# A transformer layer on one core: the first group of tokens in a fixed order, its first block loaded in halves, the array warmed by matmuls

## The chip, the cores and the metric

The kernel runs on one core of one Trainium2 chip. The metric is the device time of one execution in microseconds (us); lower is better. The kernel before took 1701.09 us (median of three runs, 1698.03 to 1702.44).

## The reference

One layer with attention and a gated feed-forward part, each between two layer norms, on 2048 tokens of width 1024 in fp32:

```python
x = x + layernorm(attn(layernorm(x)))     # 4 * 256 -> q, k, v of width 256, one head, softmax, Wo
x = x + layernorm(ffn(layernorm(x)))      # silu(x Wg^T) * (x Wu^T), then Wd^T; hidden width 2752
```

## The kernel before, in words

Matmuls take fp32r operands. To keep fp32 accuracy every operand is split into a high part, which is a cast to fp32r, and a low part, the operand minus its high part; a product is then the sum of three matmuls (`mm3`) or, for v, of one 512-column and one 256-column matmul. `split` does the cast on ACT (L109) and the subtraction on DVE (L110).

The tokens are worked in four groups of 512 (`NG`), each of four blocks of 128 tokens (`TB`). For one block, `prep1` computes the row statistics (`norm_stats`: two `bn_stats` L116, `bn_aggr` L119, the addition of epsilon L120 on DVE, a power on POOL L121), normalises the block in place (L131 on DVE), transposes it by eight PE transposes (L139) into two PSUM banks, splits those into `xT`, and loads a block of the next group into the buffer that has come free. `v_block` forms v of a block from eight chunks of `wv` (L206 and L207), adds its bias (L210, L211 on DVE) and splits the result into `vt`. `qk` (L146 to L148) forms q or k of a whole group, 24 matmuls for each of four weight blocks.

Before the first product, `load_x` queues four blocks of x on SP, and `load_wv`, `load_wqk` queue weights on ACT, through two raw buffers (`wraw`) that both use in turn. At the very start 28 PE transposes of the identity (L216, `WARM`) keep the array busy.

A planner (the tile framework's scheduler with its own cost model) chooses the order of the instructions on each engine from the program, except where `tc.keep_in_program_order` fixes an instruction to its place. Before the change the first group is not fixed; the planner mixes its blocks with each other and with statistics of the second group. Engines execute their instructions in that order.

After the four groups come the scores of 128-query blocks (`scores`, a row maximum on DVE for each of four PSUM banks), the softmax (`softmax`: four exponentials on ACT from the four banks into `p_s`), transposes of `p_s` (`turn`), products with v (`attend`), the output projection, and then the feed-forward part, most of the time (L605). The weights `wo` are split into the buffer that held `wv`, once v is done. `scores(0)` and `softmax(0)` stand, in the program, just before the last group's four `v_block`s.

Of the kernel before, what the change touches and what calls it, by code (L numbers as in the profile page):

```python
# [10 lines left out]
AF = mybir.ActivationFunctionType  # L11
ALU = mybir.AluOpType
# [3 lines left out]
P = 128  # L16
T = 2048
C = 1024
D = 256
# [5 lines left out]
TB = G // P  # L25
# [3 lines left out]
EPS = 1e-5  # L29
# [5 lines left out]
def block_kernel(ctx, tc, x, wqk, wv, bqk, bv, wo, bo, wgu, wlast, wd, out):  # L35
# [12 lines left out]
    nc = tc.nc  # L48
# [4 lines left out]
    def tl(p, shape, dt, name):  # L53
        return p.tile(shape, dt, tag=name, name=name, bufs=1)
# [3 lines left out]
    ident = tl(cpool, [P, P], F32, "ident")  # L58
    make_identity(nc, ident)
    bqk_s = tl(cpool, [P, 4], F32, "bqk_s")  # L60
    bv_s = tl(cpool, [P, D], F32, "bv_s")
    bo_s = tl(cpool, [P, C], F32, "bo_s")

    mhalf = tl(cpool, [P, 16], F32, "mhalf")[:, 0:1]
    nc.vector.memset(mhalf, -0.5)

    ys = [tl(cpool, [P, 32], F32, f"ys{i}") for i in range(2 * TB)]
# [4 lines left out]
    def small_tile():  # L72
        small_n[0] += 1
        return small[small_n[0] % NSM]

    bank_pool = pool("banks", space=PSUM)
    bank = [tl(bank_pool, [P, 512], F32, f"bank{i}") for i in range(8)]
# [22 lines left out]
    qa = tl(rpool, [P, 2, 2, 512], F32R, "qa")  # L100
# [4 lines left out]
    def f32(ap):  # L105
        return ap.bitcast(F32)

    def split(hi, lo, src, lo_engine=None):
        nc.scalar.copy(hi, src)  # L109
        (lo_engine or nc.vector).tensor_tensor(lo, src, f32(hi), ALU.subtract)  # L110

    def norm_stats(halves, pin=None):

        s = small_tile()
        for i, h in enumerate(halves):
            b = nc.vector.bn_stats(s[:, 6 * i : 6 * i + 6], h)  # L116
            if pin:
                pin(b)
        nc.vector.bn_aggr(s[:, 12:14], s[:, 0:12])  # L119
        nc.vector.tensor_scalar(s[:, 14:15], s[:, 13:14], EPS, None, ALU.add)  # L120
        nc.gpsimd.tensor_tensor(s[:, 15:16], s[:, 14:15], mhalf, ALU.pow)  # L121
        return s[:, 12:13], s[:, 15:16], s

    def norm_rows(t, scalar):

        m, r, s = norm_stats([t[:, 0:512], t[:, 512:1024]])
        if scalar:
            nc.gpsimd.tensor_scalar(s[:, 16:17], m, r, -1.0, ALU.mult, ALU.mult)
            nc.scalar.activation(t, t, AF.Identity, bias=s[:, 16:17], scale=r)
        else:  # L130
            nc.vector.tensor_scalar(t, t, m, r, ALU.subtract, ALU.mult)  # L131

    def transpose_rows(t, dst, tb, banks):

        for hf in range(2):
            b = banks[hf]
            for j in range(4):
                cb = 4 * hf + j
                nc.tensor.transpose(b[:, j * P : (j + 1) * P], t[:, cb * P : (cb + 1) * P], ident)  # L139
            src = b.rearrange("p (j t) -> p j t", j=4)  # L140
            cols = slice(tb * P, (tb + 1) * P)
            split(dst[:, 4 * hf : 4 * hf + 4, 0, cols], dst[:, 4 * hf : 4 * hf + 4, 1, cols], src)
# [11 lines left out]
    vt = a1.rearrange("p a b c -> p (a b c)").rearrange("p (k h d) -> p k h d", h=2, d=D)  # L154
    xin, wraw, qst = f4[0:4], [f4[4], f2p[1]], f2[0:2]
    vst = [f2[4][:, 0:D], f2[4][:, D:]]
    wv_s = wvo.rearrange("p a b c -> p (a b c)").rearrange("p (k h d) -> p k h d", h=2, d=D)
    wqk_pool = pool("wqk", side="right")
    wqk_s = [tl(wqk_pool, [P, 8, 2, P], F32R, f"wqk{i}") for i in range(4)]
    x0_pool = pool("x0")  # L160
    xT = [tl(x0_pool, [P, 8, 2, G], F32R, "xT0"), a2]

    def load_x(t):
        nc.sync.dma_start(xin[t % TB], x[t * P : (t + 1) * P, :])

    raw_n = [0]
    WARM = 28

    def load_wqk(i):
        r = wraw[raw_n[0] % 2].rearrange("p (c f) -> p c f", f=P)  # L170
        raw_n[0] += 1
        nc.scalar.dma_start(r, wqk[i])
        split(wqk_s[i][:, :, 0, :], wqk_s[i][:, :, 1, :], r)

    def load_wv(i):
        r = wraw[raw_n[0] % 2].rearrange("p (c f) -> p c f", f=D)
        raw_n[0] += 1
        nc.scalar.dma_start(r, wv[:, 4 * i : 4 * i + 4, :])
        split(wv_s[:, 4 * i : 4 * i + 4, 0, :], wv_s[:, 4 * i : 4 * i + 4, 1, :], r)

    def prep1(t, banks):

        r = xin[t % TB]
        norm_rows(r, False)
        transpose_rows(r, xT[(t // TB) % 2], t % TB, banks)
        if t + TB < NT:
            load_x(t + TB)
# [11 lines left out]
            nc.scalar.activation(s, b, AF.Identity, bias=bqk_s[:, i : i + 1])  # L199
            nc.sync.dma_start(q_d[g][:, i - 2, :], s)  # L200

    def v_block(g, tb, b):
        xg = xT[g % 2]
        cols = slice(tb * P, (tb + 1) * P)
        for c in range(8):
            nc.tensor.matmul(b, xg[:, c, 0, cols], wv_s[:, c, :, :].rearrange("p a f -> p (a f)"), start=(c == 0), stop=False)  # L206
            nc.tensor.matmul(b[:, D:], xg[:, c, 1, cols], wv_s[:, c, 0, :], start=False, stop=(c == 7))  # L207
        k = g * TB + tb
        s = vst[tb % 2]
        nc.vector.tensor_tensor(s, b[:, :D], bv_s, ALU.add)  # L210
        nc.vector.tensor_tensor(s, b[:, D:], s, ALU.add)  # L211
        split(vt[:, k, 0, :], vt[:, k, 1, :], s)


    for _ in range(WARM):
        nc.tensor.transpose(bank[5][:, 0:P], ident, ident)  # L216

    load_x(0)
    load_wv(0)
    load_x(1)  # L220
    load_wv(1)
    load_x(2)
    load_x(3)
    nc.scalar.dma_start(bv_s, bv.partition_broadcast(P))
    nc.scalar.dma_start(bqk_s, bqk)
    for tb in range(TB):
        prep1(tb, (bank[2 * (tb % 2)], bank[2 * (tb % 2) + 1]))
        load_wqk(tb)
        v_block(0, tb, bank[6 + tb % 2])
    nc.scalar.dma_start(bo_s, bo.partition_broadcast(P))  # L230


    qraw = f4[4].rearrange("p (d q) -> p d q", d=2)
# [65 lines left out]
    def residual(t, a, xt):  # L299

        m, r, s = norm_stats([a[:, 0:512], a[:, 512:1024]], tc.keep_in_program_order if t >= EARLY else None)
        nc.gpsimd.tensor_scalar(s[:, 16:17], m, r, -1.0, ALU.mult, ALU.mult)
        nc.scalar.activation(a, a, AF.Identity, bias=s[:, 16:17], scale=r)
        (nc.gpsimd if t >= EARLY else nc.vector).tensor_tensor(xt, xt, a, ALU.add)
        nc.sync.dma_start(x1_d[t], xt)
        m, r, s = norm_stats([xt[:, 0:512], xt[:, 512:1024]])
        nc.gpsimd.tensor_scalar(s[:, 16:17], m, r, -1.0, ALU.mult, ALU.mult)
        nc.scalar.activation(a, xt, AF.Identity, bias=s[:, 16:17], scale=r)

    for g in range(NG):  # L310
# [24 lines left out]
    for tb in range(TB):  # L335
        v_block(NG - 1, tb, bank[6 + tb % 2])
# [43 lines left out]
    L, R = slice(0, 512), slice(512, 1024)  # L380
# [22 lines left out]
    pin = tc.keep_in_program_order  # L403
# [72 lines left out]
    class Slot:  # L476
        t = None
# [421 lines left out]
    for i in range(NT):  # L899
# [28 lines left out]
        cb = i - EARLY - 3  # L928
# [121 lines left out]
```

## Time and profile before

| | us |
|---|---|
| median of three runs | 1701.09 |
| the profiled execution, its own time | 1700.9 |
| its span in the profile | 1699.1 |
| PE busy | 1669.2 |
| DVE busy | 1100.3 |
| ACT busy | 694.8 |
| POOL busy | 91.3 |

The profile shows one execution. Start times are microseconds from the start of its span; about 1.8 us lie outside it. PE is the matmul engine and PEld its weight loads, DVE the vector engine, ACT the scalar engine, POOL and SP the other two; a trailing q is an engine's own instruction queue. A busy PE may still run at half its clock; the column PEclk tells the granted share.

### The profile page before, as it was taken

What the parts mean: (1) busy time and instruction counts of PE and PEld (TensorE: products, weight loads), DVE (VectorE), ACT (ScalarE), POOL (GpSimd) and SP (SyncE); (2) the same over time, 40 slices, a digit from 0 to 9 for tenths busy, and PEclk for the clock granted to TensorE, in tenths of its full rate; (3) what the DMA queues carried; (4) which work ended last, traced back from release to release, by engine and by line L of the source; (5) the groups of instructions that cost most, each with busy time, mean ns of one, the idle gap of its engine ahead of it and who ended that gap; (6) DMA issues with size and microseconds to landing.
All of it is one profiled execution on the core that took longest, in us unless ns stands there. A gap on an engine that the chain in (4) does not pass through costs nothing.

```text
span 1699.1 us, 21099 instructions
## 1 busy us (share of the span) xinstructions
PE 1669.2 (98%) x7764; PEld 1385.5 (82%) x7764; DVE 1100.3 (65%) x1682; ACT 694.8 (41%) x1039; POOL 91.3 (5%) x118
## 2 busy tenths in 40 slices
PE   8999999999899999999999999999999999999997
PEld 6888887888678888888888888788888888888886
DVE  8643667667787777776578457866555665455458
ACT  3222445544544444443365444433333333344343
POOL 1000000000011211110000000100000000000001
PEclk9999999999999999999999999999999999999999
DMA  6221123334676566665367666633332223566654
GB/s 214 81 81 38 38 75 121 101 118 169 218 243 209 200 215 212 217 220 183 122 204 252 215 191 198 210 106 113 130 111 100 93 94 124 209 221 192 195 189 158
DMA packets 131014, 271.00 MB, mean 159 GB/s; under 512 B 13280, under 2 KB 29792, under 8 KB 130912
## 3 DMA queue, kind: packets, MB, share of 16 engines
q1 hardware_dynamic: 128176, 262.72, 46.5%
q10 hardware_dynamic: 2736, 6.95, 1.2%
q8 instruction: 60, 0.98, 0.2%
q14 instruction: 42, 0.34, 0.1%
HBM read 185.73 MB, written 83.89 MB: 159 GB/s over the span
## 4 chain that ended last, share of the span: by engine, by line
PE 92%; DVE 4%; DMA 2%; ACT 1%; issue 1%; POOL 0%; SPq 0%; POOLq 0%; DVEq 0%; ACTq 0%
PE bank L605 69%; PE bank L146 4%; PE bank L147 4%; PE bank L148 4%; PE bank L276 3%; PE bank L277 2%; PE bank L206 2%; PE bank L268 1%; PE bank L207 1%; PE bank L347 1%; PE bank L139 1%; DVE a L110 1%; DVE small L116 0%; DMA f<-xT_d 0%; DVE wvo L110 0%
## 5 line engine op out<-in xcount | busy, mean ns | idle before, releaser
L605 PE MATMUL bank<-a 128*128 128x512 f32 x1164 | 274.2, 389 | 0.0
L605 PEld LDWEIGHTS bank<-a 128*128 128x128 f32 x1164 | 218.5, 188 | 45.3
L605 PE MATMUL bank<-xb,a 128*128 128x512 f32 x912 | 212.3, 389 | 0.1
L605 PEld LDWEIGHTS bank<-xb,a 128*128 128x128 f32 x912 | 171.1, 188 | 36.0 <-ACT xi L621 0.6
L618 DVE TENSOR_TENSOR xi<-bank,xi 128x512 f32<-128x512 f32 (+1 forms) x170 | 114.0, 682 | 115.0 <-PE bank L605 70.1
L110 DVE TENSOR_TENSOR a<-f2p,a 128x1024 fp32r<-128x1024 f32 (+2 forms) x133 | 134.6, 1012 | 58.0 <-ACT a L109 54.0
L109 ACT CAST a<-f2p 128x1024 fp32r<-128x1024 f32 (+2 forms) x133 | 117.5, 884 | 131.7 <-PE bank L605 107.2
L110 DVE TENSOR_TENSOR a<-f,a 128x1024 fp32r<-128x1024 f32 (+2 forms) x91 | 89.9, 988 | 106.5 <-ACT a L109 99.8
L605 PE MATMUL bank<-wvo 128*128 128x512 f32 x612 | 149.6, 389 | 0.0
L605 PE MATMUL bank<-kx,a 128*128 128x512 f32 x612 | 146.2, 389 | 0.0
L605 PE MATMUL bank<-a,a 128*128 128x512 f32 x588 | 140.2, 390 | 3.8 <-ACT xi L661 2.6
L605 PEld LDWEIGHTS bank<-kx,a 128*128 128x128 f32 x612 | 114.9, 188 | 23.8
L605 PEld LDWEIGHTS bank<-wvo 128*128 128x128 f32 x612 | 114.9, 188 | 23.9
L605 PEld LDWEIGHTS bank<-a,a 128*128 128x128 f32 x588 | 110.2, 188 | 27.5 <-ACT xi L661 3.0
L109 ACT CAST a<-f 128x1024 fp32r<-128x1024 f32 (+2 forms) x91 | 69.5, 764 | 141.6 <-PE bank L605 110.3
L605 PE MATMUL bank<-a,wvo 128*128 128x512 f32 x444 | 106.3, 389 | 0.0
L605 PE MATMUL bank<-kx,wvo 128*128 128x512 f32 x420 | 100.1, 389 | 0.0
L605 PEld LDWEIGHTS bank<-a,wvo 128*128 128x128 f32 x444 | 83.3, 188 | 17.3
L276 PE MATMUL bank<-a,a 128*128 128x512 f32 x256 | 94.6, 403 | 2.8 <-ACT f L349 2.0
L110 DVE TENSOR_TENSOR wvo<-f,wvo 128x1024 fp32r<-128x1024 f32 (+1 forms) x52 | 60.8, 1169 | 54.9 <-ACT wvo L109 53.8
L605 PEld LDWEIGHTS bank<-kx,wvo 128*128 128x128 f32 x420 | 78.8, 188 | 16.4
L618 DVE TENSOR_TENSOR xi<-xi,xi 128x512 f32<-128x512 f32 (+1 forms) x124 | 85.3, 688 | 5.6 <-ACT xi L621 1.5
(233 smaller groups left out, 2677.5 us busy)
## 6 DMA issues: line engine op xcount, KB each, us to landing
f2p<-wgu SPq DMA_DIRECT2D x41, 512.0 KB, 5.6
hd_S<-xi SPq DMA_DIRECT2D x80, 256.0 KB, 4.4
f<-x SPq DMA_DIRECT2D x30, 512.0 KB, 3.8
hd_A<-xi SPq DMA_DIRECT2D x60, 256.0 KB, 2.0
f<-wgu SPq DMA_DIRECT2D x22, 512.0 KB, 3.5
wr<-wgu SPq DMA_DIRECT2D x21, 512.0 KB, 5.9
f<-wd SPq DMA_DIRECT2D x20, 512.0 KB, 5.0
td_T<-f SPq DMA_DIRECT2D x40, 256.0 KB, 4.6
```

The costliest lines, as they stand in the source:

```text
L109: nc.scalar.copy(hi, src)
L110: (lo_engine or nc.vector).tensor_tensor(lo, src, f32(hi), ALU.subtract)
L139: nc.tensor.transpose(b[:, j * P : (j + 1) * P], t[:, cb * P : (cb + 1) * P], ident)
L146: nc.tensor.matmul(o, w[0], m[0], start=first, stop=False)
L147: nc.tensor.matmul(o, w[0], m[1], start=False, stop=False)
L148: nc.tensor.matmul(o, w[1], m[0], start=False, stop=last)
L206: nc.tensor.matmul(b, xg[:, c, 0, cols], wv_s[:, c, :, :].rearrange("p a f -> p (a f)"), start=(c == 0), stop=False)
L207: nc.tensor.matmul(b[:, D:], xg[:, c, 1, cols], wv_s[:, c, 0, :], start=False, stop=(c == 7))
L276: nc.tensor.matmul(b, p[:, k, 0, :], vt[:, k, :, :].rearrange("p h d -> p (h d)"), start=(k == 0), stop=False)
L277: nc.tensor.matmul(b[:, D:], p[:, k, 1, :], vt[:, k, 0, :], start=False, stop=(k == NKB - 1))
L605: one = nc.tensor.matmul(o, w[i], m[j], start=first and n == 0, stop=last and n == 2, skip_group_check=chained)
L618: nc.vector.tensor_tensor(o, a, b, op)
```

## The change

It touches the stretch before the second group, and with it the planner's order of what follows.

- The first block of x is loaded in two halves of 512 columns, one queued on SP and one on ACT. The two `wv` loads stay on ACT, behind that half. The bias loads `bv`, `bqk`, `bo` and the four `wqk` loads move from ACT's queue to SP's, where they stand among the loads of x.
- A copy of one column on ACT comes first, so that ACT's function table is loaded then. A second copy makes an fp32r copy of the identity, and 40 matmuls of 128 columns on it take the place of the 28 transposes.
- DVE, ACT and PE instructions of the first group, the POOL ones apart, are fixed in the order in which they are written. The first block is normalised in halves. Blocks 2 and 3 are normalised on ACT (`normed_scalar`) instead of DVE. The v products of a block are written as all 512-column matmuls and then all 256-column ones (block 0 in two runs of four chunks).
- `v_block` of the later groups keeps its form; `norm_rows` and `norm_stats` fix their DVE instructions where they are given `pin`, which `prep1` now does in every group. `norm_stats` now fixes its last two DVE instructions too, so the late `residual` calls, which passed `pin` before, have two more fixed ones.

```diff
     def prep1(t, banks):
         r = xin[t % TB]
-        norm_rows(r, False)
+        norm_rows(r, False, tc.keep_in_program_order)
...
-    WARM = 28
+    WARM = 40
...
     def load_wqk(i):
...
-        nc.scalar.dma_start(r, wqk[i])
-        split(wqk_s[i][:, :, 0, :], wqk_s[i][:, :, 1, :], r)
+        nc.sync.dma_start(r, wqk[i])
+        tc.keep_in_program_order(nc.scalar.copy(wqk_s[i][:, :, 0, :], r))
+        tc.keep_in_program_order(nc.vector.tensor_tensor(wqk_s[i][:, :, 1, :], r, f32(wqk_s[i][:, :, 0, :]), ALU.subtract))
...
+    def v_products(g, tb, b, c0, c1, run, pin=lambda i: i):
...
+        for h, c in [(h, c) for r in range(c0, c1, run) for h in range(2) for c in range(r, r + run)]:
+            if h == 0:
+                pin(nc.tensor.matmul(b, xg[:, c, 0, cols], wv_s[:, c, :, :].rearrange("p a f -> p (a f)"), start=(c == 0), stop=False))
+            else:
+                pin(nc.tensor.matmul(b[:, D:], xg[:, c, 1, cols], wv_s[:, c, 0, :], start=False, stop=(c == 7)))
...
-    for _ in range(WARM):
-        nc.tensor.transpose(bank[5][:, 0:P], ident, ident)
-    load_x(0)
-    load_wv(0)
-    load_x(1)
-    load_wv(1)
-    load_x(2)
-    load_x(3)
-    nc.scalar.dma_start(bv_s, bv.partition_broadcast(P))
-    nc.scalar.dma_start(bqk_s, bqk)
-    for tb in range(TB):
-        prep1(tb, (bank[2 * (tb % 2)], bank[2 * (tb % 2) + 1]))
-        load_wqk(tb)
-        v_block(0, tb, bank[6 + tb % 2])
-    nc.scalar.dma_start(bo_s, bo.partition_broadcast(P))
+    nc.sync.dma_start(xin[0][:, L], x[0:P, L])
+    nc.scalar.dma_start(xin[0][:, R], x[0:P, R])
+    load_x(1)
+    for i, r in enumerate(wraw):
+        nc.scalar.dma_start(r.rearrange("p (c f) -> p c f", f=D), wv[:, 4 * i : 4 * i + 4, :])
+    load_x(2)
+    load_x(3)
+    nc.sync.dma_start(bv_s, bv.partition_broadcast(P))
+    nc.sync.dma_start(bqk_s, bqk)
+    nc.scalar.copy(ys[0][:, 0:1], mhalf)
+    warm = qa[:, 0, 0, 0:P]
+    nc.scalar.copy(warm, ident)
+    for _ in range(WARM):
+        nc.tensor.matmul(bank[5][:, 0:P], warm, warm, start=True, stop=True)
...
+    def normed_scalar(tb, st):
+        m, r, q = st
+        nc.gpsimd.tensor_scalar(q[:, 16:17], m, r, -1.0, ALU.mult, ALU.mult)
+        pin(nc.scalar.activation(xin[tb], xin[tb], AF.Identity, bias=q[:, 16:17], scale=r))
...
+    st = stats(0)
+    normed(0, L, st)
+    normed(0, R, st)
+    turn_x(0)
+    split_wv(0)
+    turned(0, 0)
+    turned(0, 1)
+    v_products(0, 0, vb[0], 0, 4, 4, pin)
+    load_x(TB)
+    st = stats(1)
+    split_wv(1)
+    v_products(0, 0, vb[0], 4, 8, 4, pin)
+    normed(1, slice(0, C), st)
+    turn_x(1)
+    st = stats(2)
+    turned(1, 0)
+    turned(1, 1)
+    v_out(0, 0, vb[0], pin)
+    v_products(0, 1, vb[1], 0, 8, 8, pin)
+    load_x(TB + 1)
+    load_wqk(0)
+    normed_scalar(2, st)
+    turn_x(2)
+    st = stats(3)
+    turned(2, 0)
+    turned(2, 1)
+    v_out(0, 1, vb[1], pin)
+    v_products(0, 2, vb[0], 0, 8, 8, pin)
+    load_x(TB + 2)
+    load_wqk(1)
+    normed_scalar(3, st)
+    turn_x(3)
+    turned(3, 0)
+    turned(3, 1)
+    v_out(0, 2, vb[0], pin)
+    v_products(0, 3, vb[1], 0, 8, 8, pin)
+    load_x(TB + 3)
+    load_wqk(2)
+    v_out(0, 3, vb[1], pin)
+    load_wqk(3)
+    pin(nc.sync.dma_start(bo_s, bo.partition_broadcast(P)))
```

`turn_x` is the eight transposes of a block, `turned` the split of one of its two banks, `stats` is `norm_stats`, `normed` the DVE normalisation, `split_wv` the split of half of `wv`, and `v_out` the part of `v_block` behind its products; all are fixed in order by `pin`.

More of the change, by code (lines that the diff above doesn't have):

```diff
@@ L118, in norm_stats, with norm_rows @@
                 pin(b)
-        nc.vector.bn_aggr(s[:, 12:14], s[:, 0:12])
-        nc.vector.tensor_scalar(s[:, 14:15], s[:, 13:14], EPS, None, ALU.add)
+        b = nc.vector.bn_aggr(s[:, 12:14], s[:, 0:12])
+        if pin:
+            pin(b)
+        b = nc.vector.tensor_scalar(s[:, 14:15], s[:, 13:14], EPS, None, ALU.add)
+        if pin:
+            pin(b)
         nc.gpsimd.tensor_tensor(s[:, 15:16], s[:, 14:15], mhalf, ALU.pow)
         return s[:, 12:13], s[:, 15:16], s
-    def norm_rows(t, scalar):
-        m, r, s = norm_stats([t[:, 0:512], t[:, 512:1024]])
+    def norm_rows(t, scalar, pin=None):
+        m, r, s = norm_stats([t[:, 0:512], t[:, 512:1024]], pin)
         if scalar:
@@ L171, in load_wqk @@
         raw_n[0] += 1
-        nc.scalar.dma_start(r, wqk[i])
-        split(wqk_s[i][:, :, 0, :], wqk_s[i][:, :, 1, :], r)
[L175 to L179, printed above, removed]
+        nc.sync.dma_start(r, wqk[i])
+        tc.keep_in_program_order(nc.scalar.copy(wqk_s[i][:, :, 0, :], r))
+        tc.keep_in_program_order(nc.vector.tensor_tensor(wqk_s[i][:, :, 1, :], r, f32(wqk_s[i][:, :, 0, :]), ALU.subtract))
     def prep1(t, banks):
         r = xin[t % TB]
-        norm_rows(r, False)
+        norm_rows(r, False, tc.keep_in_program_order)
         transpose_rows(r, xT[(t // TB) % 2], t % TB, banks)
@@ L200, in qk @@
             nc.sync.dma_start(q_d[g][:, i - 2, :], s)
-    def v_block(g, tb, b):
+    def v_products(g, tb, b, c0, c1, run, pin=lambda i: i):
         xg = xT[g % 2]
         cols = slice(tb * P, (tb + 1) * P)
-        for c in range(8):
-            nc.tensor.matmul(b, xg[:, c, 0, cols], wv_s[:, c, :, :].rearrange("p a f -> p (a f)"), start=(c == 0), stop=False)
-            nc.tensor.matmul(b[:, D:], xg[:, c, 1, cols], wv_s[:, c, 0, :], start=False, stop=(c == 7))
+        for h, c in [(h, c) for r in range(c0, c1, run) for h in range(2) for c in range(r, r + run)]:
[3 more added lines that the diff above has]
+                pin(nc.tensor.matmul(b[:, D:], xg[:, c, 1, cols], wv_s[:, c, 0, :], start=False, stop=(c == 7)))
@@ L208, in v_block, with v_out @@
+    def v_out(g, tb, b, pin=lambda i: i):
         k = g * TB + tb
         s = vst[tb % 2]
-        nc.vector.tensor_tensor(s, b[:, :D], bv_s, ALU.add)
-        nc.vector.tensor_tensor(s, b[:, D:], s, ALU.add)
-        split(vt[:, k, 0, :], vt[:, k, 1, :], s)
-    for _ in range(WARM):
-        nc.tensor.transpose(bank[5][:, 0:P], ident, ident)
-    load_x(0)
-    load_wv(0)
+        pin(nc.vector.tensor_tensor(s, b[:, :D], bv_s, ALU.add))
+        pin(nc.vector.tensor_tensor(s, b[:, D:], s, ALU.add))
+        pin(nc.scalar.copy(vt[:, k, 0, :], s))
+        pin(nc.vector.tensor_tensor(vt[:, k, 1, :], s, f32(vt[:, k, 0, :]), ALU.subtract))
@@ L220, in block_kernel, with v_block @@
+    def v_block(g, tb, b):
+        v_products(g, tb, b, 0, 8, 1)
+        v_out(g, tb, b)
+    pin = tc.keep_in_program_order
+    L, R = slice(0, 512), slice(512, 1024)
+    nc.sync.dma_start(xin[0][:, L], x[0:P, L])
+    nc.scalar.dma_start(xin[0][:, R], x[0:P, R])
     load_x(1)
-    load_wv(1)
+    for i, r in enumerate(wraw):
+        nc.scalar.dma_start(r.rearrange("p (c f) -> p c f", f=D), wv[:, 4 * i : 4 * i + 4, :])
     load_x(2)
     load_x(3)
-    nc.scalar.dma_start(bv_s, bv.partition_broadcast(P))
@@ new lines, in hi, with lo, split_wv, turned @@
+    def hi(dst, src):
+        pin(nc.scalar.copy(dst, src))
+    def lo(dst, src, h):
+        pin(nc.vector.tensor_tensor(dst, src, f32(h), ALU.subtract))
+    def split_wv(i):
+        r = wraw[i].rearrange("p (c f) -> p c f", f=D)
+        w = wv_s[:, 4 * i : 4 * i + 4]
+        hi(w[:, :, 0, :], r)
+        lo(w[:, :, 1, :], r, w[:, :, 0, :])
+    def turned(tb, h):
+        b = bank[2 * (tb % 2) + h].rearrange("p (j t) -> p j t", j=4)
+        d = xT[0][:, 4 * h : 4 * h + 4, :, tb * P : (tb + 1) * P]
+        hi(d[:, :, 0, :], b)
+        lo(d[:, :, 1, :], b, d[:, :, 0, :])
@@ new lines, in turn_x, with stats, normed @@
+    def turn_x(tb):
+        for h in range(2):
+            for j in range(4):
+                cb = 4 * h + j
+                pin(nc.tensor.transpose(bank[2 * (tb % 2) + h][:, j * P : (j + 1) * P], xin[tb][:, cb * P : (cb + 1) * P], ident))
+    def stats(tb):
+        return norm_stats([xin[tb][:, L], xin[tb][:, R]], pin)
+    def normed(tb, h, st):
+        r = xin[tb][:, h]
+        pin(nc.vector.tensor_scalar(r, r, st[0], st[1], ALU.subtract, ALU.mult))
+    def normed_scalar(tb, st):
+        m, r, q = st
+        nc.gpsimd.tensor_scalar(q[:, 16:17], m, r, -1.0, ALU.mult, ALU.mult)
+        pin(nc.scalar.activation(xin[tb], xin[tb], AF.Identity, bias=q[:, 16:17], scale=r))
@@ new lines, in block_kernel @@
+    vb = bank[6:8]
+    st = stats(0)
[19 more added lines that the diff above has]
+    load_wqk(0)
```

## Prediction

> **What bounds the kernel now.** I read the page first: shares of busy time, then the slices.
>
> ```profile
> span 1699.1 us, 21099 instructions
> PE 1669.2 (98%) x7764; PEld 1385.5 (82%) x7764; DVE 1100.3 (65%) x1682; ACT 694.8 (41%) x1039; POOL 91.3 (5%) x118
> ...
> PE   8999999999899999999999999999999999999997
> ```
>
> PE is idle for only 1699.1 - 1669.2 = 29.9 us, so a change that leaves the matmuls alone moves time only through gaps of PE and its clock. Windows of 20 us place them: 6.4 us before 40 us, about 4 between 160 and 300, about 8.5 between 420 and 500, 1.3 near 1105, and the tail, 10.6. The first group is next, in windows of 5 us (columns: width, busy time and count of PE, PEld, DVE, ACT, POOL, then clock, DMA share, GB/s).
>
> ```profile
> 0.00:5.00 5.00, 3.64 (x17) 3.64 (x18) 0.06 (x1) 0.00 (x0) 0.70 (x6) 1.00 0.59 174
> 5.00:10.00 5.00, 2.96 (x19) 2.73 (x18) 3.15 (x6) 2.33 (x2) 0.55 (x1) 1.00 1.00 393
> 10.00:15.00 5.00, 3.75 (x13) 2.30 (x10) 5.00 (x9) 2.02 (x3) 0.00 (x0) 0.53 1.02 393
> 15.00:20.00 5.00, 4.03 (x19) 3.16 (x20) 5.00 (x14) 1.70 (x3) 1.97 (x3) 0.78 0.48 129
> 20.00:25.00 5.00, 4.87 (x33) 4.00 (x33) 5.00 (x10) 3.13 (x6) 1.64 (x2) 1.00 0.71 240
> 25.00:30.00 5.00, 4.33 (x28) 3.32 (x26) 5.00 (x11) 1.54 (x2) 0.00 (x0) 1.00 0.75 259
> 30.00:35.00 5.00, 5.00 (x24) 4.13 (x23) 4.59 (x9) 2.02 (x3) 0.00 (x0) 1.00 0.52 145
> ```
>
> DVE is full from 10 to 30 us and PE is full only from 30 on: DVE bounds the first group. The chain of waits says the same.
>
> ```profile
> 0.73 5.80 DMA f<-wv
> ...
> 6.92 1.28 ACT L109
> ...
> 8.21 1.05 ACT wvo L109
> ...
> 9.29 1.23 DVE wvo L110
> ...
> 25.62 0.60 DVE xT L110
> ...
> 26.26 0.39 PE bank L207
> ...
> 30.20 0.24 PE bank L147
> ```
>
> The wv load, the table load (6.92), the wv split, then DVE up to 26 us, then PE. The clock column (0.53, 0.78) shows the array at half speed from 10.3 to 17.1, which DVE hides.
>
> **What the Trainium skill says.** "TensorE: Matmul & The Clock Gate", Part 1, says that the array drops to half clock after an idle window of about 3.4 us and returns after a busy one. The trace agrees: half-microsecond windows put the drop at 10.3 and the return at 17.1, two such windows, although 28 transposes ran from 1.4 to 7.3. "ScalarE: Activation LUTs", What ACT_TABLE_LOAD costs, gives 1283 ns; here 1.28 us, and nothing of the drain that the page adds. "Trainium Kernel Development and Optimization", Key Constraints, says that SP's and ACT's transfers share the same 16 DMA engines; the trace has them at a share of 1.00 and 393 GB/s, so two queues alone add no bandwidth.
>
> **The change, part by part.** I walk the first group in its new fixed order with durations of before: statistics 1.28 + 0.20 + 0.15 and 0.55 on POOL; DVE normalisation 0.81, ACT's (L303) 1.24; casts 1.05 (1024 columns), 0.59 (512, PSUM), 0.41 (256); subtractions 1.22, 0.69, 0.42; v's two additions 0.41 + 0.40; PE 0.23 per 512 columns, 0.87 for eight transposes, and about 0.2 until the last result. Neighbours on DVE and ACT overlap by 0.1; a semaphore costs 0.05.
>
> Loads. The DMA engines had moved 0.52 MB by 3.9 us and 1.57 MB by 6.95, and a landing is seen about 0.45 later. With x's halves first on both queues, block 0 lands at about 4.4 (was 6.1), the first wv half, now behind it and level with block 1, at 7.4 (was 6.5). The table load, moved ahead of the data, takes 1.28 off the wv cast: 7.4 instead of 8.2. Warming: after three DMA issues on ACT (to 2.1), the table load and two short copies, the fp32r copy is ready at about 3.9; 40 matmuls at a cold 0.107 (the 768 cold columns at 12.7 took 0.64) end by 8.2.
>
> Block 0 is normalised at 6.8 to 7.5, transposed from 8.2; the first v half waits for wv's subtraction until 9.8. DVE then runs without a gap: two subtractions, statistics, second wv subtraction to 13.65. The second v half starts at 13.75, block 1's transposes at 15.1, its v ends at 19.4. For blocks 2 and 3 a loop forms: transposes, cast, two subtractions, v's additions on DVE, then on ACT, in order, the v cast, the wqk cast (1.05) and the normalisation (1.24) before the next transposes. The waiting normalisation holds PE; POOL's two added products end at 17.3 and 23.9, before ACT is free for it. The loop gives transposes at 21.0 and 27.1, 6.1 apart, and block 3's v products at 28.5.
>
> Before, at 30.20, all but block 3's v and 94 of 96 q/k products was done, with eight transposes of group 2 (0.87) and two q/k matmuls (0.46) beyond; the equal state is at 28.87. The start gains 0.4. If block 0 lands only at 6.0, the walk gives 29.1, a loss of 0.2; a wv half at 6.5 gives 28.0, a gain of 0.9.
>
> Clock. Between the two v halves PE now idles from 11.4 to 13.7. I charge 1.0, between 0 and 4: a half-clock window of 3.4 us costs up to 1.7 where PE bounds, and two can fall in this stretch. The 28 transposes removed and the 40 matmuls hide under the loads.
>
> SP's queue: wqk loads wait there for raw buffers, group 2's x loads behind them. wqk 0 to 3 issue at 9.8, 13.7, 21.1 and 27.2 and are needed at 18.7, 24.9, 30.8 and 35.3; x of block 4 is needed only at 39. Both are costed at nothing, hidden by that slack; without it, 4 to 5 us of landing would show. The later bo load serves the attention projection, first used at 196 us: nothing.
>
> Later groups. Group 2's statistics now follow on DVE at 39; PE wants that block at 46. In the built order of group 3, its last block's normalisation stands behind a v addition, two residuals and a POOL power; my walk has it 0.7 late, its cast 0.4 more: 1.0 lost, from 0 to 2.
>
> **Start of attention.** Here the planner's new order matters most. Before, the first softmax ran under v products:
>
> ```profile
> 157.12 0.39 PE L148 MATMUL bank<-kx,qa 128*128 128x512 f32 x1
> ...
> 158.66 0.69 ACT L259 ACTIVATE p_s<-bank,ys 128x512 f32<-128x512 f32 x1 [5.13 <-DVE ys L257]
> ...
> 162.99 0.60 PE L268 MATMUL bank<-ident,p_s 128*128 128x128 f32 x4
> ```
>
> In the changed program the last scores stand behind all q/k products, with nine v matmuls left as cover:
>
> ```
> PE:  scores(0,3) x5; v block 15 x9; turn(0,0)
> DVE: max of bank3; wo half 0 low; v 15 add; wo half 1 low; softmax scale
> ACT: q casts; wo half 0/1 high; exp(0,0)
> ```
>
> With 0 at the first of the five scores, they end at 1.15 and v at 2.65. ACT's second wo cast needs v's sixth chunk, 2.2, and ends at 3.3; DVE, after the v addition at 3.7, subtracts until 4.85, scales until 5.05; the exponential takes 0.69, so the transposes start near 5.85. PE waits 3.1 us. Before, PE lost 0.9 around 178 here; I let that go: net 2.2, from 0 to 3.5. The rest of attention keeps a steady order with 4.8 us of PE work over each softmax; nothing, give or take 2.
>
> Sum against the profiled execution: -0.4 + 1.0 + 1.0 + 2.2 = +3.8, so 1700.9 + 3.8 = **1704.7 us**. The profiled time stands 0.2 below the median. The start lies within about 5.1 us, 0.3%, which is what a measurement of this kernel can tell from no change.
>
> **Rivals.** *No change that can be told* (0.47): the sum above, with own range 1699 to 1706.
>
> *Slower* (0.38): the array falls to half clock in the first group. The page's 10.3 to 17.1 speaks for it: 40% busy in the window before was too little. The new order leaves 11.4 to 13.7 empty and pauses of 1.6 and 1.8 us before blocks 2 and 3. Against it, 40 matmuls leave it warm at 8.2. A cold window on the transposes of block 1 costs 2.1 through the loop, one at 28 us costs 1.7: 3.8 in place of 1.0 gives 1700.9 + 6.6 = 1707.5. It decides from 2.3 us of clock loss on.
>
> *Faster* (0.15): the planner's new order removes gaps of attention, 0.9 near 178 and 3.1 between 200 and 300, and one of the 1.6 waits between 420 and 500, adds none, the array stays warm and wv lands at 6.5: 1700.9 - 0.9 - 4.0 - 1.6 = 1694.4. The cover that I miss at attention's start speaks against it.
>
> *Not what it says*: the halves may not land earlier; the wv split bounds then as now, so that costs the 0.6 between 28.5 and 29.1, within the first case.
>
> **How the numbers follow.** Faster by over 0.3%: 0.15; within: 0.47; slower: 0.38. The range reaches from the faster case's near edge, 1696.5, to the slower case with attention's upper bound, 1707.5 + 1.3 and 1 of other gaps: 1710.
>
> **What would show it.** In the profile after: PE full from 28 to 29; the wv cast at 7.4 with no table load ahead; the transposes of blocks 2 and 3 released by ACT, 6 us apart; PE waiting about 3 us for p_s near 160; the clock column near 14. Wrong if PE is full by 25 us, if no wait of over 1 us stands ahead of the first p_s transposes, or if the gaps between 420 and 500 change by over 3 us.

## The result, and the profile after

Over six executions each, the changed kernel took 1707.61 us (median; 1705.73 to 1709.31) and the kernel before 1699.20: a ratio of 1.0043 with a 95% interval of 1.003 to 1.0056, so 0.43% slower. (The ratios in this document are the recorded estimates over the single executions; dividing these two medians would give 1.0049.) The profiled execution after took 1707.8 by its own time, 6.9 more than the profiled one before, where the prediction's sum was +3.8.

The page after, its lines on the span, on busy time and PE's slices:

```profile
span 1705.7 us, 21134 instructions
PE 1676.1 (98%) x7776; PEld 1393.2 (82%) x7776; DVE 1099.5 (64%) x1681; ACT 698.7 (41%) x1043; POOL 90.1 (5%) x120
...
PE   8999999999999999999999999999999999999997
```

PE's idle time is 1705.7 - 1676.1 = 29.6 us, against 29.9 before. By the page nothing was gained or lost in waiting: PE is busy 6.9 us longer, although the layer's own matmuls are the same. The extra busy time is in the 40 warm matmuls, which last longer than the 28 transposes did, and in matmuls at half clock. This is the first thing to see: a busy share cannot tell work from filler.

The first group after, in windows of 5 us (columns as in the prediction):

```profile
0.00:5.00 5.00, 1.13 (x5) 1.13 (x6) 0.79 (x3) 1.67 (x3) 0.70 (x6) 1.00 0.63 213
5.00:10.00 5.00, 5.00 (x25) 5.00 (x25) 2.06 (x6) 1.05 (x1) 0.55 (x1) 1.00 0.95 340
10.00:15.00 5.00, 5.00 (x23) 4.68 (x23) 1.77 (x2) 1.15 (x3) 0.00 (x0) 1.00 0.59 208
15.00:20.00 5.00, 2.90 (x12) 2.27 (x11) 4.43 (x8) 0.97 (x2) 1.48 (x1) 0.90 0.42 120
20.00:25.00 5.00, 5.00 (x24) 4.30 (x24) 3.47 (x8) 1.30 (x3) 0.82 (x2) 0.76 0.48 161
25.00:30.00 5.00, 3.12 (x19) 2.43 (x18) 4.09 (x8) 3.45 (x5) 0.70 (x2) 0.92 0.39 127
30.00:35.00 5.00, 4.48 (x22) 3.55 (x20) 2.72 (x6) 3.12 (x5) 0.12 (x1) 0.74 0.45 132
```

DVE, which was full from 10 to 30 us before, is nowhere full. PE is full from 5 to 15, and DVE is busy for only 2.06 and 1.77 of 5 us there. PE is full for good only from 35, where it was 30 before. The timeline of PE says what it does (start, length, line, tiles, shape, count; in brackets the idle time ahead and what ended it):

```profile
3.87 8.80 PE L240 MATMUL bank<-qa 128*128 128x128 f32 x40 [3.87 <-ACT qa L238]
12.47 1.93 PE L265 MATMUL bank<-ident,f 128*128 128x128 f32 x8
14.22 1.80 PE L207 MATMUL bank<-wvo,xT 128*128 128x512 f32 x4
...
18.58 1.75 PE L207 MATMUL bank<-wvo,xT 128*128 128x512 f32 x4 [2.10 <-DVE wvo L246]
...
20.98 1.73 PE L265 MATMUL bank<-ident,f 128*128 128x128 f32 x8
...
27.43 1.10 PE L265 MATMUL bank<-ident,f 128*128 128x128 f32 x8 [1.65 <-ACT f L277]
28.77 3.42 PE L207 MATMUL bank<-wvo,xT 128*128 128x512 f32 x8 [0.24 <-ACT xT L243]
...
33.68 1.09 PE L265 MATMUL bank<-ident,f 128*128 128x128 f32 x8 [0.30 <-ACT f L277]
35.02 1.20 PE L207 MATMUL bank<-wvo,xT 128*128 128x512 f32 x4 [0.24 <-ACT xT L243]
```

DVE's timeline has the normalisation of block 0:

```profile
6.66 1.00 DVE L272 TENSOR_SCALAR f<-f,small 128x512 f32<-128x512 f32 x2 [0.67 <-POOL small L125]
```

The 40 matmuls take 8.80, 0.22 each. Block 0 was normalised by 7.66, so its transposes (L265) are 4.8 late, and no bracket tells so, since PE was not idle: work in front of other work on the same engine is a wait that no list of waits contains. When they do start they run at half speed, 1.93 for eight, where a full clock gives about 1.0. The chain of waits puts the matmuls on the path, and shows further on what stands between the blocks:

```profile
3.87 8.80 PE bank L240 x40
12.67 1.74 PE bank L265 x8
...
25.19 1.05 ACT wqk L177
26.27 1.22 DVE wqk L178
27.49 1.21 DVE small L116 x2
...
31.45 1.04 ACT wqk L177
32.49 1.15 ACT f L277
...
33.68 0.67 PE bank L265 x4
```

Block 3's v products start at 35.02. The equal state of the kernel before was at 28.87, so the start costs 6.15. At the start of attention, just before 180 us, the list of PE's waits (waited for, us in total, times, longest) has:

```profile
PE bank L358 <- ACT p_s L349: 2.8, 1, 2.8
```

### The profile page after: what moved, and what is told of

The parts are those of the page before. It is cut to its first block, busy times and chain, and to the rows that moved or that the text cites. A ratio compares the mean times of both kernels' runs of the same rounds, so it can differ in the third digit from the quotient of the medians.

```text
span 1705.7 us, 21134 instructions
## 1 busy us (share of the span) xinstructions
PE 1676.1 (98%) x7776; PEld 1393.2 (82%) x7776; DVE 1099.5 (64%) x1681; ACT 698.7 (41%) x1043; POOL 90.1 (5%) x120
## 4 chain that ended last, share of the span: by engine, by line
PE 90%; DVE 4%; DMA 2%; ACT 2%; issue 1%; ACTq 0%; POOL 0%; DVEq 0%; SPq 0%; POOLq 0%
PE bank L695 67%; PE bank L150 4%; PE bank L152 4%; PE bank L151 4%; PE bank L366 3%; PE bank L367 2%; PE bank L358 1%; PE bank L207 1%; PE bank L437 1%; PE bank L209 1%; DVE a L110 1%; PE bank L143 1%; PE bank L240 1%; DMA f<-xT_d 0%; DVE wvo L110 0%
## 5 line engine op out<-in xcount | busy, mean ns | idle before, releaser
L110 DVE TENSOR_TENSOR a<-f2p,a 128x1024 fp32r<-128x1024 f32 (+2 forms) x133 | 134.5, 1012 | 58.9 <-ACT a L109 55.1
L110 DVE TENSOR_TENSOR a<-f,a 128x1024 fp32r<-128x1024 f32 (+1 forms) x75 | 83.2, 1109 | 105.6 <-ACT a L109 99.0
L109 ACT CAST a<-f 128x1024 fp32r<-128x1024 f32 (+1 forms) x75 | 63.0, 840 | 110.7 <-PE bank L695 110.3
L110 DVE TENSOR_TENSOR wvo<-f,wvo 128x1024 fp32r<-128x1024 f32 (+1 forms) x51 | 59.5, 1167 | 53.8 <-ACT wvo L109 53.1
```

## The experiments

The theory after the result: the warm matmuls hold PE past the moment at which it has real work, and the loss at attention's start is a second cost that stands by itself. The rivals: the loop through ACT would hold the start whatever the warming, or the warming was needed and the slow array is the cost. A time below is a median, a ratio is against the kernel before, timed on the same chip. Some differences between two runs are of medians from different chips; the kernel before took 1698.96 to 1699.58 on these, so a few tenths in them mean nothing. "Cover" is work that an engine can do in a stretch in which it would otherwise wait.

**Run 1: fewer warm matmuls.**

```diff
-    WARM = 40
+    WARM = 18
```

> 18 warm matmuls instead of 40; every other instruction of every engine stands where it stood in the changed kernel. Theory A (the warm matmuls hold PE past the moment at which block 0 is normalised): at 0.22 each they end near 7.9 instead of 12.7, block 0 is transposed at about 8.0 (12.47 with 40), block 3's v products start some 3 to 5 us earlier than 35.0 (30 to 32), and the time falls by 3 to 5 us below the changed kernel. Rival B (the loop through ACT, in which the normalisation of blocks 2 and 3 stands behind a v cast and a wqk cast, sets the start): the first transposes move, but block 3's v stays within 1 us of 35.0 and the time within 1 us. Rival C (the 40 matmuls are what keeps the clock up later): the clock column shows more half-speed windows before 35 us and the time rises by 1.7 for each.

Measured: 1702.36 us, ratio 1.0016 (1.001 to 1.0023), 5.3 below the changed kernel. PE's timeline:

```profile
3.88 4.11 PE L240 MATMUL bank<-qa 128*128 128x128 f32 x18 [3.88 <-ACT qa L238]
7.78 1.93 PE L265 MATMUL bank<-ident,f 128*128 128x128 f32 x8
...
24.42 1.09 PE L265 MATMUL bank<-ident,f 128*128 128x128 f32 x8 [1.64 <-ACT f L277]
...
30.69 1.09 PE L265 MATMUL bank<-ident,f 128*128 128x128 f32 x8 [1.87 <-ACT f L277]
32.02 1.19 PE L207 MATMUL bank<-wvo,xT 128*128 128x512 f32 x4 [0.24 <-ACT xT L243]
```

Block 0 is transposed 4.7 earlier and block 3's v starts 3.0 earlier, with the same order of instructions on every engine but for one product of the scores near 187 us. Theory A holds, with both numbers at the edge of what was expected; rival C falls, since the time went down. The loop (rival B) is not all of it, but 32.02 is still 3.15 behind the kernel before, so it can be the rest.

Only 3.0 of the 5.3 is seen at the start. Set side by side, the two profiles keep this distance to about 445 us; it is 3.9 at 470, 4.1 at 1080 and 5.9 at 1112, behind a wait of 1.2 that the changed kernel has and this run lacks. Run 2 has such a wait (1.0). Why the later gaps differ isn't shown.

**Run 2: none at all** (`WARM = 0`).

> No warm matmul at all; the order of the rest is the changed kernel's but for a handful of places. Theory A: block 0 is transposed at about 7.8, the array is at half clock there exactly as with 40 (0.215 a transpose), block 3's v starts within 1 us of the kernel with 18, and the time within 1.5 us of it: the warm matmuls buy nothing. Rival C (they do warm the array, late): the first release of the clock comes 3 us or more later than with 18, and the time is 1.7 to 3.4 us above it.

Measured: 1703.10 us, ratio 1.0024 (1.0016 to 1.0032). Block 0 is transposed at 7.39, again in 1.97, and block 3's v starts at 32.00. The matmuls on the identity bought nothing that these intervals can tell (theory A; rival C wanted at least 1.7 more than run 1).

**Runs 3 and 4: cover for the first softmax.** The v products of the last group held behind the four scores on PE, with 40 and with 18 warm matmuls:

```diff
     for tb in range(TB):
-        v_block(NG - 1, tb, bank[6 + tb % 2])
+        v_products(NG - 1, tb, bank[6 + tb % 2], 0, 8, 1, pin)
+        v_out(NG - 1, tb, bank[6 + tb % 2])
```

> The v products of the last group are held on PE behind all four scores of the first turn, as they stood in the kernel before; the warm matmuls stay at 40. Theory: the 2.8 us for which PE waits for the first p_s goes (under 0.3), and with it the half-clock window after it (0.91 between 170 and 190 us), so the time falls by 2.8 to 4.5 us below the changed kernel, while the start stays as it was (block 3's v at 35.0). Rival: the wait only moves to the next turn, or to the v copies of the last group that attention needs, and the time falls by less than 1 us.

> 18 warm matmuls and the held v products together. If the start and the start of attention are two independent costs, the gains of the two single edits add: 6 to 9 us below the changed kernel, that is 1699 to 1702 us, level with the kernel before. If attention absorbs either (as it gave back about 4 us of what was lost ahead of it in the changed kernel), the sum falls short by 2 us or more.

Measured: 1713.34 us, ratio 1.0073 (1.0061 to 1.0085), and 1707.84, 1.0044 (1.0032 to 1.0056). Both lose 5.5 to 5.7 against their partner without the cover. The wait for p_s did go, but in the list of PE's waits of the first of them, between 100 and 180 us, stand:

```profile
PE bank L150 <- DVE a L110: 2.6, 1, 2.6
PE bank L143 <- DVE f L135: 1.8, 2, 1.5
```

As I read these waits, the v products had covered the casts before the first scores, and moved behind them they left that place open. Besides, PE's idle time between 180 and 300 us, 0.3 in the changed kernel, is 3.8. The theory of a cost that can be bought off alone fell.

**Run 5: the normalisation first.** With 18 warm matmuls. `v_out` is cut into its additions on DVE (`v_adds`) and the copy and subtraction (`v_keep`), so that ACT's normalisation can stand ahead of the copy and of the wqk cast:

```diff
     turn_x(1)
-    st = stats(2)
+    st2, st3 = stats(2), stats(3)
     turned(1, 0)
     turned(1, 1)
-    v_out(0, 0, vb[0], pin)
+    normed_scalar(2, st2)
+    v_adds(0, 0, vb[0], pin)
     v_products(0, 1, vb[1], 0, 8, 8, pin)
     load_x(TB + 1)
-    load_wqk(0)
-    normed_scalar(2, st)
     turn_x(2)
-    st = stats(3)
     turned(2, 0)
     turned(2, 1)
-    v_out(0, 1, vb[1], pin)
+    normed_scalar(3, st3)
+    v_adds(0, 1, vb[1], pin)
+    v_keep(0, 0, pin)
+    load_wqk(0)
...
```

> 18 warm matmuls, and in the fixed order ACT's normalisation of blocks 2 and 3 stands directly behind the xT casts of the block before it, ahead of v's copy and the wqk cast; statistics of block 3 follow those of block 2. Theory A (with the warming out of the way it is this loop that sets the start): from the durations of the kernel with 18, transposes of block 2 at 22.4 (24.4 there), of block 3 at 26.4 (30.7), block 3's v products at 27.6 (32.0), which is 1.3 before the equal state of the kernel before; the time falls by 3 to 5 us below the kernel with 18, to 1697 to 1699.5. Rival B (the slow array sets the start, not the order): block 3's v moves by less than 2 us. Rival C (PE is earlier at block 3 but then waits for wqk casts that now stand later): idle of PE between 28 and 40 rises by what the start gains.

Measured: 1698.41 us, ratio 0.9998 (0.9989 to 1.0006), 4.0 below run 1. Its PE timeline:

```profile
22.00 1.04 PE L272 MATMUL bank<-ident,f 128*128 128x128 f32 x8
...
26.19 1.03 PE L272 MATMUL bank<-ident,f 128*128 128x128 f32 x8
27.46 1.20 PE L207 MATMUL bank<-wvo,xT 128*128 128x512 f32 x4 [0.24 <-ACT xT L250]
```

No bracket stands before the transposes any more: PE no longer waits for ACT. 22.00, 26.19 and 27.46 against the expected 22.4, 26.4 and 27.6. Rival C falls too: PE's idle time between 28 and 40 us, 2.1 in run 1, is nothing here. The order on ACT was the second cost of the start, hidden behind the first. This run, which has fewer warm matmuls and the new order on ACT, is back at the time of the kernel before.

**Run 6: the early table load alone, in the kernel before.**

```diff
+    nc.scalar.copy(ys[0][:, 0:1], mhalf)
     for _ in range(WARM):
```

> The kernel before, with one more ACT copy ahead of the first loads' use, so that the table is loaded at once; no other instruction moves on any engine. If the table load (1.28 at 6.92 in the chain of waits) is worth what the chain shows, the wv cast goes to 6.9, DVE's row of work starts 1.28 earlier and the time falls by about 1.3. My theory: nothing (within 0.3 in the profile's start, the wv subtraction still at 9.3), because DVE's normalisation of block 0, which stands ahead of that subtraction and ends at 9.31, is as late as the cast is.

Measured: 1698.61 us, ratio 1.0 (0.9991 to 1.001). Its wv cast stands at 7.21, 1.0 earlier, and DVE's timeline is:

```profile
8.84 0.81 DVE L131 TENSOR_SCALAR f<-f,small 128x1024 f32<-128x1024 f32 x1 [0.67 <-POOL small L121]
9.56 1.22 DVE L110 TENSOR_TENSOR wvo<-f,wvo 128x1024 fp32r<-128x1024 f32 x1
```

The subtraction (L110) starts the moment DVE is through with the normalisation, and not earlier than before (9.29), although its cast had been done for 1.3 us. (Block 0's statistics started 0.34 later in this execution, 6.45 against 6.11, which is why it is even a little later.) The chain of waits shows one path; a second one, here DVE's statistics and normalisation, was exactly as late.

**Run 7: the old warming in the changed kernel.** 28 transposes of the identity instead of the 40 matmuls.

```diff
-    WARM = 40
+    WARM = 28
...
-        nc.tensor.matmul(bank[5][:, 0:P], warm, warm, start=True, stop=True)
+        nc.tensor.transpose(bank[5][:, 0:P], ident, ident)
```

> The changed kernel, warmed by the 28 transposes of the identity that the kernel before used instead of 40 matmuls; the planner orders later groups somewhat differently, so the start is what is read. Theory A (the transposes release the clock and, needing no copy, start at 1.4 and end by 7.4): block 0's eight transposes start at 7.7 and take 1.0, not 1.93; block 1's start near 16.8 (17.8 with 18 matmuls) and take 0.9 to 1.0, block 3's v products start at 30 to 30.5, 1.5 to 2 earlier than with 18 matmuls. Rival B (PE's idle stretches between 9 and 15 make it slow again whatever came first): block 1's transposes take 1.7 to 1.9 and block 3's v starts within 0.7 of 32.0.

Measured: 1705.34 us, ratio 1.0038 (1.0024 to 1.0053). Its PE timeline:

```profile
1.35 5.33 PE L240 MATMUL bank<-ident 128*128 128x128 f32 x28 [1.35 <-POOL ident masks.py:199]
7.10 1.11 PE L265 MATMUL bank<-ident,f 128*128 128x128 f32 x8 [0.41 <-DVE f L272]
...
15.97 1.91 PE L265 MATMUL bank<-ident,f 128*128 128x128 f32 x8
...
28.86 1.39 PE L265 MATMUL bank<-ident,f 128*128 128x128 f32 x8 [1.87 <-ACT f L277]
30.19 2.07 PE L207 MATMUL bank<-wvo,xT 128*128 128x512 f32 x4
```

Both theories were half right: the transposes release the clock (block 0's take 1.11), PE then idles for 2.3 us twice and block 1's are slow again (1.91). Block 3's v starts at 30.19, 1.8 ahead of run 1, but its products run at half speed, so that the q/k product that follows at 34.90 there follows at 34.34 here: 0.6 is left. The time is nevertheless 3.0 above run 1. The largest difference between the two profiles is in attention, which the planner put in another order. Three windows of 120 us tell it, the changed kernel, the kernel before, and this run:

```profile
180.00:300.00 120.00, 119.74 (x659) 101.47 (x658) 78.99 (x168) 61.46 (x129) 8.99 (x22) 0.99 0.23 77
```

```profile
180.00:300.00 120.00, 116.94 (x645) 98.11 (x645) 80.54 (x167) 59.47 (x123) 9.80 (x24) 1.00 0.25 80
```

```profile
180.00:300.00 120.00, 117.07 (x641) 98.54 (x641) 79.19 (x164) 57.67 (x119) 8.67 (x21) 1.00 0.23 72
```

PE's idle time there is 0.3, 3.1 and 2.9 us. Runs 1, 2 and 5, in which the planner's order stays close to the changed kernel's, have 0.3 at most; this run has the wait of 2.8 for p_s as well as the gaps. So the order of attention that came with the change saves 2.8, and it isn't the price of the wait ahead of it.

**Runs 8 and 12: what the warm matmuls do to the clock.** In the changed kernel, 20 of 512 columns (run 8, four copies of the identity side by side), and 40 of 256 (run 12, two copies). The edit of run 12:

```diff
-    nc.scalar.copy(warm, ident)
+    wide = qa[:, 0, 0, 0 : 2 * P]
+    for k in range(2):
+        nc.scalar.copy(wide[:, k * P : (k + 1) * P], ident)
...
-        nc.tensor.matmul(bank[5][:, 0:P], warm, warm, start=True, stop=True)
+        nc.tensor.matmul(bank[5][:, 0 : 2 * P], warm, wide, start=True, stop=True)
```

> 20 warm matmuls of 512 columns in place of 40 of 128, which at half clock hold PE about as long (20 x 0.43 = 8.6, from about 4.6). Read for the start alone: the later order differs. Theory A (fp32r at 128 columns runs at half the column rate, and such matmuls do not count as work for the clock): the later ones take 0.215 instead of 0.43, PE is free near 11 instead of 13.2, block 0's transposes take 1.0. Rival B (no fp32r matmul on the identity warms the array): all 20 take 0.43 and the transposes 1.9.

> 40 warm matmuls of 256 columns instead of 128; read for the start alone, the later order differs. Theory (a 128-column fp32r matmul takes the time of a 256-column one, 0.215 at half clock, with the array at work half of that time, and it is this half that keeps the clock from being released): the first ones take 0.215 each as before, the later ones about 0.11, PE is free by 9.5 to 10.5 instead of 12.5, and block 0's transposes take about 1.0 instead of 1.93. Rival (what matters is something else, such as the weight load that each one brings, which is the same here): all 40 take 0.215 to 12.7 and the transposes take 1.9.

The PE timelines of the two, 512 columns first:

```profile
4.47 6.74 PE L242 MATMUL bank<-qa 128*128 128x512 f32 x20 [4.47 <-ACT qa L240]
11.05 1.03 PE L267 MATMUL bank<-ident,f 128*128 128x128 f32 x8
```

```profile
4.08 7.58 PE L242 MATMUL bank<-qa 128*128 128x256 f32 x40 [4.08 <-ACT qa L240]
11.49 1.04 PE L267 MATMUL bank<-ident,f 128*128 128x128 f32 x8
```

One time each, 1707.70 and 1706.43; only the start is read. With 256 columns the matmuls run 0.21 apart up to about 9.8 and 0.12 apart afterwards; with 512 columns, 0.43 apart up to about 8.5 and 0.23 afterwards. In both, block 0 is then transposed at full clock (1.04 and 1.03). With 128 columns they run 0.21 apart to the end, and the transposes behind them are slow (1.93): the clock had not been released. So one of 128 columns takes the time of one of 256 at half clock, and a row of them does not release the clock, while the wider ones do; both rivals fall. How the hardware counts this the runs don't show. PE was free later than I expected in run 12 (11.5 against 9.5 to 10.5).

**Run 9: half the cover.** Run 5, with only the first of the last group's four v blocks held:

```diff
-        v_block(NG - 1, tb, bank[6 + tb % 2])
+        v_products(NG - 1, tb, bank[6 + tb % 2], 0, 8, 1, *([pin] if tb == 0 else []))
+        v_out(NG - 1, tb, bank[6 + tb % 2])
```

> The kernel of the run with the normalisation first, and of the last group's v products only the first block held behind the scores of the first turn: 25 v matmuls then stand between scores(0,3) and the first p_s transposes instead of nine, and one block of 16 stays where it fills the time before the first scores. Theory (the start of attention costs 2.8 us of waiting and about 1.7 of the half clock after it, and cover pays if it isn't taken from a place that needs it): the wait for p_s falls under 0.5, no wait of over 1 us comes up between 120 and 160 us, the clock column stays at 1.0, and the time falls by 3 to 4.5 us, to 1694 to 1695.5. Rival (as when all four blocks were held): attention between 180 and 300 us goes back to the gaps of the kernel before (2.7 us more) or a wait of 2 to 3 us appears near 130, and the time falls by less than 1.5 or rises.

Measured: 1696.77 us, ratio 0.9985 (0.9979 to 0.9992), 1.6 below run 5. The list of PE's waits between 90 and 200 us:

```profile
PE bank L143 <- DVE f L135: 2.4, 1, 2.4
```

The wait for p_s is gone, the gaps after 180 stay away (0.2), but a wait of 2.4 for a block's normalisation, at 136 to 138 us, takes its place, much as the rival had it. Neither had the time right.

**Runs 10 and 11: the weights of v earlier.** Run 11 is run 1 with wv asked for ahead of block 1 of x, a half on each queue; run 10 is run 9 with that and with the 28 transposes of run 7.

```diff
-    load_x(1)
-    for i, r in enumerate(wraw):
-        nc.scalar.dma_start(r.rearrange("p (c f) -> p c f", f=D), wv[:, 4 * i : 4 * i + 4, :])
+    nc.sync.dma_start(wraw[0].rearrange("p (c f) -> p c f", f=D), wv[:, 0:4, :])
+    nc.scalar.dma_start(wraw[1].rearrange("p (c f) -> p c f", f=D), wv[:, 4:8, :])
+    load_x(1)
```

> The kernel with normalisation first and one block held, and besides it 28 transposes of the identity as warming instead of 18 matmuls, and wv's two halves asked for ahead of block 1 of x, one on each queue. Expected if each of the two is worth what the single runs showed: wv's first cast at about 7.4 (8.3 to 8.8), the first v products near 9.5, warm, block 3's v products at 25 to 26.5 (27.5), and the time 1 to 2 us below the kernel with one block held. Rival: a wv half earlier only brings block 1 of x later (its statistics wait on DVE ahead of wv's second subtraction), or PE's longer idle ahead of block 1 slows the array as it did after 28 transposes, and block 3's v stays at 27 or later with no gain in time.

> 18 warm matmuls, and wv's two halves asked for ahead of block 1 of x, one on each queue; read for the start alone, the later order differs. If the wv landing (cast at 8.7) is what set the first v products, the cast comes at about 7.4 and everything to block 3's v is 1.2 to 1.4 earlier than with 18 matmuls (32.0). Rival: block 1 of x lands later by as much and takes it back at the second v half, and block 3's v stays within 0.4.

Measured: run 11 has the wv cast at 7.03 (8.73 in run 1) and block 3's v at 28.70 (32.02); 1699.72 us in its one timing. 1.7 of the 3.3 is the cast; the rest goes with a full clock on the second v half and block 1's transposes, which run 1 did not have. Run 10 takes 1693.87 us, ratio 0.9966 (0.9954 to 0.9978), faster than the kernel before by about 5 us and than the changed one by about 14. It is 2.9 below run 9, where 1 to 2 was expected. Its PE timeline:

```profile
7.24 1.11 PE L272 MATMUL bank<-ident,f 128*128 128x128 f32 x8
9.54 1.16 PE L207 MATMUL bank<-wvo,xT 128*128 128x512 f32 x4 [1.19 <-DVE wvo L253]
...
13.42 1.84 PE L207 MATMUL bank<-wvo,xT 128*128 128x512 f32 x4 [2.25 <-DVE wvo L253]
...
26.01 1.19 PE L207 MATMUL bank<-wvo,xT 128*128 128x512 f32 x4 [0.24 <-ACT xT L250]
```

The first v products (9.54) and block 3's v (26.01) came as expected. Block 1 of x did not come late: its statistics on DVE waited for nothing (10.51, directly behind a subtraction). The rival's other half came in part: behind a pause of 2.25 the second v half is slow again (1.84). What each of the two edits is worth in time wasn't measured apart.

## Why the prediction was right or wrong

The direction was half right: I called it slower on the mean and gave slower 0.38, but held a change within 0.3% likelier (0.47). The sum put +3.8 where +6.9 came, inside the range. The rival's 1707.5 is almost the time measured, but for a different mechanism, and that is no credit to it. That the time fell inside the range is luck in the same way: the upper part of the range was built from a cold clock, not from the matmuls that filled it, and attention gave some of the loss back.

| step | predicted | measured |
|---|---|---|
| block 0 lands | 4.4 | 4.27 |
| fp32r copy ready | 3.9 | 3.87 |
| block 0 normalised | 6.8 to 7.5 | 6.66 to 7.66 |
| warm matmuls end | 8.2 | 12.67 |
| wv cast | 7.4 | 8.77 |
| first, second v half | 9.8, 13.75 | 14.22, 18.58 |
| transposes of blocks 1, 2, 3 | 15.1, 21.0, 27.1 | 20.98, 27.43, 33.68 |
| block 3's v | 28.5 | 35.02 |
| later groups | 1.0 | 0.8 idle (0.60 and 0.24, in 100 to 160) |
| PE's wait for p_s | 3.1, net 2.2 | 2.8, net 1.9 |
| rest of attention | 0, give or take 2 | -2.8 idle in 180 to 300 |

**The step that failed is "40 matmuls at a cold 0.107 ... end by 8.2".** I had the price by dividing the time of 768 columns by six pieces of 128; a matmul of 128 columns takes 0.22. A nearer price stood in the profile before, the 28 transposes of 128 columns, 0.213 each:

```profile
1.36 5.97 PE L216 MATMUL bank<-ident 128*128 128x128 f32 x28 [1.36 <-POOL ident masks.py:199]
```

The walk then kept its other steps in their order, each late: from block 0's transposes on by 4.3 to 6.6. Run 1 shows what 22 of the 40 were worth, 3.0 us at the start and 5.3 in the median, and run 2 that nothing stood against it. "TensorE: Matmul & The Clock Gate" of the Trainium skill, Part 1, gives 106.7 ns for 128 columns on a cold array, too; no run here shows that for fp32r, and the measurement decides.

**wv's landing** was off by 1.4 and wrong the same way, but in the changed kernel the warm matmuls hid it. It came into view in run 1, and runs 10 and 11 took it away. **The table load** counted as 1.28 off that cast: right for the cast, worth nothing in run 6.

**The clock.** I charged 1.0 at the start. By the pace of equal matmuls, block 0's transposes and first v half, block 1's transposes and block 2's v ran slow. Take the walk's lags: 4.3 at block 0's transposes, 4.8 at the second v half, 5.9 at block 1's transposes, 6.5 at block 3's v. The first 4.3 are the held PE; the other 2.2 go with slow stretches on the path, and are near the 2.1 and 1.7 of the rival's single windows. Run 1's walk agrees: 32.02 against 28.5, where 1.3 is there at the second v half (wv) and 2.2 comes after it, with slow matmuls there too. That the rest is the clock alone is argued, not shown. Runs 1 and 4 put a number on one such stretch: with the same instructions, and the second v half started at 15.06 and 15.13, its products ran slow in run 1 and fast in run 4, and block 3's v came at 32.02 and 30.95. "Against it, 40 matmuls leave it warm at 8.2" failed outright: at 12.7 they had not released it. My "the trace agrees" was too much as well. The drop at 10.3 did not follow an idle window: PE was busy for 1.4 of the 3.4 us before it, as it was for 1.3 and 1.5 before the two drops at the changed kernel's start (19.0 and 29.2). So a window in which PE works part of the time can bring the drop.

**The loop** between blocks 2 and 3, 6.1 apart by the walk, came at 6.25, released by ACT as said. What I missed is that it could be broken by the order alone (run 5).

**The start of attention** was read rightly from the built order: 2.8 of 3.1, though at 177 to 180 us and not near 160. Two neighbours of it were not: a half-clock stretch follows the wait (clock 0.93 between 180 and 200 us, about 1.6 lost with the 0.99 before it), and the 3.1 us of gaps between 180 and 300, which I named in the rival *faster* and left out of the sum, went away. The first is uncharged, the second uncredited; they come to -1.2 together.

**420 to 520 us**: idle time fell from 8.46 to 6.46, under my bound of 3, and 1.7 of half clock came in (0.91 between 440 and 460): nothing, as costed. With the tail behind 1680 us, idle for 9.35 us instead of 9.72, I get 6.15 + 0.8 + 1.9 + 1.6 - 2.8 - 2.0 + 1.7 - 0.4 = 6.95, a little more than the 6.6 between the two spans, and I don't place the rest. The tail of 10.6 in the prediction was misread, from a window that reaches past the span's end; its wait of 3.1 is 3.2 by its own figures (5.85 - 2.65). The tail is no part of the sum, and the wait moves it by 0.1.

Of the signs named, the wv cast at 7.4 and PE full from 28 to 29 failed, and both point at the start; the 6 us between blocks 2 and 3 and the wait for p_s came.

## What to carry to other kernels

Filler on an engine, work that only fills its time, is a wait that no list shows: compare the time at which the first real operand is ready (here 7.66 on DVE) with the filler's end (12.67), and price the filler from an instruction of the same type and width. When a chain of waits names a cost, look for the second path that is as late before counting it as a gain. Work that is moved to cover one wait uncovers the place that it came from, so look there first. With an order written by hand, ask of each engine's queue what stands ahead of the instruction that PE waits for.

## What the runs showed of the hardware

- fp32r matmuls of 128 columns on the identity ran 0.21 apart, as far apart as those of 256 columns at half clock, and 40 of them in a row, 8.8 us, did not release the clock; 40 of 256 released it after about 5.7 us, 20 of 512 after about 4.1 (runs 12 and 8).
- Transposes of the identity did release it: 28 took 5.33 us in run 7, the last of them 0.11 apart instead of 0.21, and block 0's eight then 1.11 instead of 1.93. "TensorE: Matmul & The Clock Gate", Part 4, says that transposes do not count as busy in the same way; for these fp32 transposes the runs say otherwise.
- The clock column reads 1.00 from 0 to 15 us after, while eight transposes took 1.93. Here it told nothing of the start; the pace of equal instructions did.
- Where the slow windows fall differs between executions. Runs 1 and 4 have the same first 30 us of instructions, yet the first v half took 2.05 in one and 1.17 in the other. Block 3's v came at 32.02 and 30.95. A difference of about 1 us between two single profiles of the start is therefore no finding.
